# Streaming attention over 8,192 context rows: keys and values kept in DRAM and fetched per unit, 20 block-aligned units in place of 24

## The chip, the cores and the metric

The kernel runs on one core of a Trainium2 chip. The metric is the device time in microseconds. A core has TensorE (PE, with its weight loads PEld), VectorE (DVE), ScalarE (ACT), GpSimd (POOL) and SyncE (SP), which here issues nearly all DMAs; each works through its own queue in order. PE writes its results to PSUM, here in banks of 128 x 512 float32.

## What is computed

The reference is one perceiver layer in float32: a cross attention, a stack of eight linear attention blocks with feed-forward parts, and a sparse feed-forward part. The change touches the cross attention only:

```python
xn = layer_norm(x, gamma_x, beta_x)          # x: 8192 context rows of 512
ln = layer_norm(latents, gamma_l, beta_l)    # 512 latent rows
q = (ln @ Wq).reshape(b, m, h, d)            # 8 heads of 64
k_x, v_x = split(xn @ Wkv);  k_l, v_l = split(ln @ Wkv)
k_x = rope_rotate_k(k_x)
k = concatenate([k_x, k_l]);  v = concatenate([v_x, v_l])
attn = softmax(einsum('bhid,bhjd->bhij', q * scale, k))
out = einsum('bhij,bhjd->bhid', attn, v) @ Wo
```

So 512 queries look at 8,704 keys, in eight heads; the scores don't fit on the chip.

## The kernel before

The heads are taken in four pairs. The 8,704 keys are 17 blocks of 512 (block 0 is that of the latents, 1 to 16 are the context), or 68 chunks of 128. For each pair the softmax is an online one: its 68 chunks are cut into **units**, and behind each unit the running maximum, the weighted sum of values and the sum of exponentials of the pair are brought up to date.

For a block `b`, `fetch_block` loads the rows, `moments_of`, `roots_of` and `centre` normalize them (the root iteration is a chain of small POOL operations), `transpose_rows` turns them on PE, `keys_of(b, j)` projects keys (four pieces j; two pieces make two pairs, multiplied by cosines and sines on DVE, combined on POOL in L254 and L255, and moved by eight small DMAs of SP into the key tiles, L262), and `values_of(b, t)` projects values (four pieces t), which ACT copies out of PSUM in four parts, one for each pair (L270). Keys and values lie in SBUF tiles of 128 x 512 from the pool `x_kv`, which has 27 of them.

For a unit `u` of a pair, in this order:

- `score(u, i)` for its chunks i: two matmuls (pc, one for each head), two copies from PSUM by ACT (L382), and the running maximum over chunks by DVE (mx, L386 and L388). Five PSUM banks (`ps_s`) serve scores, projections and transposes together.
- `maxima(u)`: eight PE transposes (pmx), then reductions by DVE give the new row maxima `mrow`. For a pair that has been met before, POOL takes the difference between old and new maxima (alpha, L406) and ACT its exponential (L407), which is the factor by which the older sums shrink.
- `maxima_rows(u)`: eight PE transposes (mbc) spread the maxima over partitions.
- `exponentials(u, i)`: DVE subtracts (L439), ACT takes the exponential (L440), POOL adds the chunks up (es, L448 and L450).
- `shrink(u)`: eight PE matmuls (pa, L427) spread the factor over partitions, DVE multiplies the older sums `oT` by it (L432).
- `weigh(u, i)`: two PE matmuls (po, L460) weigh the values; behind the last chunk DVE adds to `oT` (L490).
- `sums(u)`: two PE matmuls with ones (pd, L499), then again an addition to `oT`.

The last unit doesn't use es; its sums are formed by PE directly. At a pair's last unit `sums_by_query` and `ones_over` turn the sums into factors (psr, pb), and `project` multiplies by Wo.

The order of all this on PE is written out by hand: the list `steps` holds the chunks, two to a step, 136 steps in all, and the dictionary `todo` holds what else belongs to each step; `rank` sorts the pieces inside a step. `end[u]` is the step of a unit's last scores. Blocks 2 to 16 are spread over eight steps each. The other engines and SP are ordered by the planner of the language, by priority and by the times at which it expects inputs, except where `issue_after` pins an instruction behind another.

Before the change the units grow by 3.25 chunks a time: there are 24 of them, of 4, 6, 9, 12, 12, then mostly 13, and at the end 10, 7 and 4 chunks, and they begin at any chunk of a block.

```python
    STEP = 3.25
    while min(met) < NCHUNK:
        p = k % NPAIR
        upto = min(NCHUNK, int(3 + STEP * k)) if k else 4
```

Of the kernel before, what the change touches and what calls it, by code (L numbers as in the profile page):

```python
# [16 lines left out]
P = 128  # L17
D = 512
# [36 lines left out]
def perceiver_kernel(  # L55
# [85 lines left out]
    kvp = pool("x_kv", 27, stack=xa)  # L141
    sp = pool("x_s", 18, stack=xa)
# [69 lines left out]
    k_sb, v_sb, xT, part, rows_of, trigs = {}, {}, {}, {}, {}, {}  # L212
# [24 lines left out]
    def keys_of(b, j):  # L237
# [18 lines left out]
        for p in (j - 1, j):  # L256
            k_sb[b, p] = kv_tile(f"k{b}_{p}")
            for h in range(2):
                src = slice((p % 2 * 2 + h) * H2, (p % 2 * 2 + h + 1) * H2)
                for i, half_of in enumerate((lo, hi)):  # L260
                    o = h * HD + i * H2
                    nc.sync.dma_start(out=k_sb[b, p][o : o + H2, :], in_=half_of[src, :])  # L262

    def values_of(b, t):
        pv = bank("pv")
        projected(pv, lambda dc: xT[b, dc][:, t * P : (t + 1) * P], lambda dc: wkv[:, 1, dc, :])
        for p in range(NPAIR):
            if t == 0:
                v_sb[b, p] = kv_tile(f"v{b}_{p}")
            nc.scalar.copy(v_sb[b, p][:, t * P : (t + 1) * P], pv[:, p * P : (p + 1) * P])  # L270
# [63 lines left out]
    STEP = 3.25  # L334
    units, met, k = [], [0] * NPAIR, 0
    while min(met) < NCHUNK:
        p = k % NPAIR
        upto = min(NCHUNK, int(3 + STEP * k)) if k else 4
# [16 lines left out]
    for b in range(2, NBLK + 1):  # L355
# [8 lines left out]
        for j, (f, i) in enumerate(pieces, 1):  # L364
            at(begin + j * gap, f, b, i)
        for e, f, *a in normalizing(b + 1) if b < NBLK else ():
            at(begin + e, f, *a)
    at(begin + 8 * gap, values_of, NBLK, TT - 1)
    pieced = set(todo)

    scores, mx, mrow, alpha, mbc, es, po = {}, {}, {}, {}, {}, {}, {}

    def score(u, i):
# [3 lines left out]
        for h in range(2):  # L377
            hs = slice(h * HD, (h + 1) * HD)
            nc.tensor.matmul(pc[h], k_sb[b, p][hs, o : o + P], qT[hs, p, :], start=True, stop=True)  # L379
# [10 lines left out]
    def maxima(u):  # L390
# [13 lines left out]
        if p in mrow:  # L404
            a = alpha[u] = small.tile([P, 2 * TT], F32, tag="alpha", name="alpha", bufs=4)
            nc.gpsimd.tensor_tensor(a, mrow[p], new, ALU.subtract)  # L406
            nc.scalar.activation(a, a, AF.Exp)  # L407
        mrow[p] = new

# [10 lines left out]
    def shrink(u):  # L420

        p = units[u][0]
        pa = bank("pa")
        for qc in range(TT):
            for h in range(2):
                c = h * TT + qc
                nc.tensor.matmul(  # L427
                    pa[h * HD : (h + 1) * HD, qc * P : (qc + 1) * P],
                    alpha[u][:, c : c + 1].to_broadcast([P, HD]), ident,
                    start=True, stop=True,  # L430
                )
        nc.vector.tensor_tensor(  # L432
            oT[p], oT[p], pa.unsqueeze(1).to_broadcast([P, 2, T]), ALU.mult
        )

    def exponentials(u, i, late=False):
# [6 lines left out]
        if i == 1:  # L443
            es[u] = (
                xpool.tile([P, 2, T], F32, tag="es", name="es") if u % 2 or units[u][2] < NCHUNK else
# [6 lines left out]
    def weigh(u, i):  # L452
# [6 lines left out]
        for h in range(2):  # L459
            nc.tensor.matmul(  # L460
                po[u][h * HD : (h + 1) * HD, :],
                v_sb[b, p][:, t * P + h * HD : t * P + (h + 1) * HD],
# [68 lines left out]
    for u, n in enumerate(size):  # L531
        at(end[u], maxima if end[u] in pieced else late_maxima, u)
        at(end[u] + 1, maxima_rows, u)
        if units[u][1]:
            at(end[u] + 2, shrink, u)
        span = size[u + 1] if u + 1 < len(size) else n
        first = last + 1 if u + 2 < len(size) else 0
        for i in range(n):
            d = end[u] + 1 + i * span // n // 2
            at(d, late_exponentials if d in end[-3:] else exponentials, u, i)  # L540
            last = max(d + 1, first)
# [840 lines left out]
```

## Time and profile before

| | us |
|---|---|
| median of three runs (2570.17 to 2570.89) | 2570.39 |
| the profiled execution | 2571.29 |
| its span, first to last instruction | 2569.2 |
| from the first score to the last weighing of the cross attention | 86.32 to about 1211.4 |
| PE, DVE, ACT, POOL busy in 212.15 to 1012.20 | 780, 575, 488, 522 |
| DMA share in that stretch | 0.14 |

In the profile's rows "out<-in" names tiles of the program, "x8" counts instructions merged into one row, and a bracket gives the idle time of the engine before the row and what ended it. A float32 matmul stands in the rows as two instructions, so the two matmuls of a score are "x4"; a transpose is one. A group of 16 "pa" is one shrink.

### The profile page before, as it was taken

The numbers are of one execution on the slowest core, as the hardware profiler recorded it, in microseconds if no ns is written. First come the engines' busy times: TensorE is split into PE (matmuls) and PEld (weight loads), VectorE is DVE, ScalarE is ACT, GpSimd is POOL, SyncE is SP. The second block draws the span as 40 slices with busy tenths as digits, with TensorE's granted clock in tenths as the row PEclk, the third lists the DMA queues.
The fourth block names the chain that finished last, engine by engine and source line by source line (L and its number), as shares of the span: only waits on it lengthen the run. The fifth ranks groups of instructions, "written<-read, shape, count | busy, mean of one in ns | idle before, by whom it ended". The sixth has DMA issues, their size and how long they took to land.

```text
span 2569.2 us, 33740 instructions
## 1 busy us (share of the span) xinstructions
PE 2501.5 (97%) x11560; PEld 1471.0 (57%) x11560; DVE 1746.6 (68%) x3680; ACT 1202.3 (47%) x2285; POOL 1263.4 (49%) x1422
## 2 busy tenths in 40 slices
PE   8999999999999999998999999999999999999998
PEld 4433333334333333333588686886868878687764
DVE  4466767766777776886675767757576575766764
ACT  3465656665566665663433415334153441524303
POOL 0255665666567666775144452544525354263512
PEclk9999999999999999998999999999999999999999
DMA  3111111111111111010522223222222323223235
GB/s 134 42 44 52 29 41 42 42 40 43 34 42 41 42 42 42 9 42 17 193 95 93 72 79 106 95 95 70 95 95 90 95 86 97 92 74 99 66 110 203
DMA packets 98380, 187.49 MB, mean 73 GB/s; under 512 B 10336, under 2 KB 10464, under 8 KB 98208
## 3 DMA queue, kind: packets, MB, share of 16 engines
q1 hardware_dynamic: 88496, 167.29, 20.3%
q10 hardware_dynamic: 8688, 15.94, 2.0%
q0 software_dynamic: 1024, 2.10, 0.3%
q8 instruction: 92, 1.51, 0.2%
q14 instruction: 80, 0.66, 0.1%
HBM read 162.22 MB, written 1.05 MB: 64 GB/s over the span
## 4 chain that ended last, share of the span: by engine, by line
PE 78%; DVE 9%; ACT 5%; issue 4%; POOL 2%; DMA 0%; SPq 0%; DVEq 0%; POOLq 0%; ACTq 0%
PE pb L846 14%; PE ps L635 13%; PE pw L730 9%; PE pv L231 7%; PE pk L231 6%; PE ps L730 6%; PE po L460 6%; PE pc L379 6%; DVE sc L439 4%; PE po L1009 4%; ACT sc L382 2%; ACT sc L440 2%; DVE mx L388 1%; PE pt L218 1%; PE pf L939 1%
## 5 line engine op out<-in xcount | busy, mean ns | idle before, releaser
L450 POOL TENSOR_TENSOR es<-es,sc 128x1024 f32<-128x1024 f32 x222 | 526.1, 2370 | 110.5 <-ACT sc L440 99.9
L388 DVE TENSOR_TENSOR mx<-pc,mx 128x512 f32<-128x512 f32 x448 | 283.3, 684 | 186.5 <-ACT sc L382 186.3
L440 ACT ACTIVATE sc<-sc 128x1024 f32<-128x1024 f32 x272 | 288.4, 1065 | 249.2 <-DVE sc L439 238.1
L382 ACT COPY sc<-pc 128x512 f32<-128x512 f32 x544 | 284.4, 600 | 81.3 <-PE pc L379 67.6
L439 DVE TENSOR_TENSOR sc<-sc,mbc 128x1024 f32<-128x1024 f32 x272 | 319.4, 1209 | 3.7 <-PE mbc L416 2.2
L379 PE MATMUL pc<-qT,k 64*128 64x512 f32 x1088 | 290.9, 621 | 5.8 <-DVE sin L249 2.3
L460 PE MATMUL po<-sc,v 128*64 128x512 f32 x1088 | 263.0, 604 | 0.2 <-DVE mx L388 0.2
L231 PE MATMUL pk<-xn,wkv 128*64 128x512 f32 (+1 forms) x856 | 250.6, 604 | 8.2 <-ACT v L270 3.4
L231 PE MATMUL pv<-wkv,xn 128*64 128x512 f32 (+1 forms) x808 | 248.0, 598 | 7.7 <-DVE sin L249 2.6
L379 PEld LDWEIGHTS pc<-qT,k 64*128 64x128 f32 x1088 | 101.4, 186 | 189.0 <-issue 80.9
L1019 ACT ACTIVATE h<-h,col 128x256 f32<-128x256 f32 x192 | 103.9, 577 | 220.5 <-DVE h L779 151.0
L903 ACT ACTIVATE g<-g 128x512 f32<-128x512 f32 x64 | 39.9, 630 | 344.7 <-DVE g L863 218.7
L730 PE MATMUL pw<-curT,cur 128*128 128x256 f32 (+1 forms) x896 | 177.3, 350 | 0.1
L231 PEld LDWEIGHTS pk<-xn,wkv 128*64 128x64 f32 (+1 forms) x856 | 85.0, 153 | 160.8 <-issue 114.1
L231 PEld LDWEIGHTS pv<-wkv,xn 128*64 128x64 f32 (+1 forms) x808 | 86.6, 155 | 150.8 <-issue 110.8
L812 POOL TENSOR_TENSOR sh<-h 128x128 f32<-128x128 f32 x120 | 83.4, 695 | 176.7 <-PE pb L846 172.1
L986 POOL TENSOR_TENSOR y<-qf,y 128x512 f32<-128x512 f32 x32 | 44.5, 1391 | 243.9 <-DVE y L985 243.9
L730 PEld LDWEIGHTS pw<-curT,cur 128*128 128x128 f32 x896 | 150.2, 190 | 16.9 <-DVE curT L723 0.2
L863 DVE TENSOR_TENSOR g<-g,pb 128x256 f32<-128x256 f32 x135 | 50.0, 417 | 159.7 <-PE pb L846 159.2
L717 POOL TENSOR_TENSOR cur<-w 128x256 f32<-128x256 f32 x128 | 93.5, 741 | 118.5 <-DVE g L904 74.9
L460 PEld LDWEIGHTS po<-sc,v 128*64 128x64 f32 x1088 | 73.6, 138 | 135.2 <-issue 120.0
L846 PE MATMUL pb<-tw,sh 128*128 128x256 f32 x540 | 136.2, 379 | 0.0
(220 smaller groups left out, 4639.7 us busy)
## 6 DMA issues: line engine op xcount, KB each, us to landing
w<-in_wf SPq DMA_DIRECT2D x64, 1024.0 KB, 5.2
k<-cos SPq DMA_DIRECT2D x272, 64.0 KB, 2.0
cb<-in_cx SPq DMA_DIRECT2D x62, 256.0 KB, 3.9
row<-in_rows ACTq DMA_DIRECT2D x48, 256.0 KB, 4.7
f<-in_f SPq DMA_DIRECT2D x10, 1024.0 KB, 5.3
tg<-in_trig SPq DMA_DIRECT2D x16, 512.0 KB, 3.6
wk<-in_wk SPq DMA_DIRECT2D x8, 1024.0 KB, 5.2
wq<-in_wq SPq DMA_DIRECT2D x8, 1024.0 KB, 5.1
```

What stands on the lines that cost most here:

```text
L231: nc.tensor.matmul(ps[o : o + n, :], lhs(dc)[:, o : o + n], rhs(dc), start=(dc == 0), stop=(dc == DC - 1))
L379: nc.tensor.matmul(pc[h], k_sb[b, p][hs, o : o + P], qT[hs, p, :], start=True, stop=True)
L382: copied[0] = nc.scalar.copy(sc[:, h, :], pc[h])
L388: behind[0] = nc.vector.tensor_tensor(mx[u][:, h, :], pc[h], mx[u][:, h, :], ALU.max)
L439: nc.vector.tensor_tensor(sc, sc, mbc[u], ALU.subtract)
L440: nc.scalar.activation(sc, sc, AF.Exp)
L450: nc.gpsimd.tensor_tensor(es[u], es[u], sc, ALU.add)
L460: nc.tensor.matmul(po[u][h * HD : (h + 1) * HD, :], v_sb[b, p][:, t * P + h * HD : t * P + (h + 1) * HD], scores[u, i][:, h, :], start=(i ...
L635: nc.tensor.matmul(ps[:, t0 : t0 + n], w[:, dc, c0 : c0 + P], xT[:, dc, t0 : t0 + n], start=(dc == 0), stop=(dc == DC - 1),)
L730: nc.tensor.matmul(ps, lhs[:, k], rhs[:, k], start=(k == 0), stop=(k == 1))
L846: nc.tensor.matmul(ps[i], lhs, rhs, start=(q == 0 and i in (1, 2, 6, 5, 4)), stop=(q == self.N - 1 and i in (1, 2, 7, 3, 4)),)
L1019: nc.scalar.activation(h, h, AF.Gelu_apprx_tanh, bias=col[:, c : c + 1])
```

## The change

Keys and values are no longer kept in SBUF. Keys go from the rope tiles to DRAM tiles, values are copied by ACT in one instruction into a small tile `vs` and stored to DRAM as well. Each unit loads the key blocks it needs (`load_keys`, three steps before the first score on them) and the value blocks (`load_values`, two steps before the first weighing, in runs of 512 bytes), all by SP. The pool `x_kv` falls from 27 to 9 tiles, and the score tiles rise from 18 to 22.

Units now begin and end at block borders: 20 units of 4, 8 and 12, then fourteen of 16, and at the end 12, 8 and 4 chunks. The number of steps stays 136. With units of 16 the ends and beginnings of units fall on the same two of the eight steps of every block.

The factor: its difference is taken by DVE at the end of `maxima`. The exponential comes a step later, in the new `factor`, which also stores the 128 x 8 factors transposed to DRAM and loads them back twice, each time as one row of 512 broadcast to 64 partitions (`abc`). `shrink` then has no matmuls; DVE multiplies by `abc`. For units of 16 chunks it comes three steps after the unit's end in place of two, for shorter ones two steps after.

The sums and what follows them come a step later (not for the last two units), and the tile es has two buffers. The pieces of the last block come one step earlier, its last values two steps earlier.

```diff
--- before.py
+++ after.py
@@ -138,8 +138,9 @@
     xnp = pool("x_feat", 4, stack=xa)
     cbp = pool("x_rows", 4, stack=xa)
     xpool = pool("xattn", 1, stack=xa)
-    kvp = pool("x_kv", 27, stack=xa)
-    sp = pool("x_s", 18, stack=xa)
+    kvp = pool("x_kv", 9, stack=xa)
+    sp = pool("x_s", 22, stack=xa)
+    dram = pool("x_dram", 1, DRAM, stack=xa)
     ps_s = pool("ps_s", 5, PSUM, stack=xa)
     ps_m = pool("ps_m", 1, PSUM, stack=xa)
     ps_o = pool("ps_o", 1, PSUM, stack=xa)
@@ -209,7 +210,8 @@
     oT = [xpool.tile([P, 2, T], F32, tag=f"oT{p}", name=f"oT{p}") for p in range(2)]
     oT += [x_sb[:, 2 * i : 2 * i + 2, :] for i in range(2)]
     H2 = HD // 2
-    k_sb, v_sb, xT, part, rows_of, trigs = {}, {}, {}, {}, {}, {}
+    k_dr, v_dr, xT, part, rows_of, trigs = {}, {}, {}, {}, {}, {}
+    kt, vt_ = {}, {}
     def transpose_rows(b, dc, gcol, bcol):
         tiles = rows_of[b]
@@ -254,20 +256,33 @@
             nc.gpsimd.tensor_tensor(lo, lo, part["sin1"], ALU.subtract)
             nc.gpsimd.tensor_tensor(hi, hi, part["sin0"], ALU.add)
         for p in (j - 1, j):
-            k_sb[b, p] = kv_tile(f"k{b}_{p}")
+            k_dr[b, p] = dram.tile([P, BLK], F32, name=f"k{b}_{p}")
             for h in range(2):
                 src = slice((p % 2 * 2 + h) * H2, (p % 2 * 2 + h + 1) * H2)
                 for i, half_of in enumerate((lo, hi)):
                     o = h * HD + i * H2
-                    nc.sync.dma_start(out=k_sb[b, p][o : o + H2, :], in_=half_of[src, :])
+                    nc.sync.dma_start(out=k_dr[b, p][o : o + H2, :], in_=half_of[src, :])
     def values_of(b, t):
         pv = bank("pv")
         projected(pv, lambda dc: xT[b, dc][:, t * P : (t + 1) * P], lambda dc: wkv[:, 1, dc, :])
-        for p in range(NPAIR):
-            if t == 0:
-                v_sb[b, p] = kv_tile(f"v{b}_{p}")
-            nc.scalar.copy(v_sb[b, p][:, t * P : (t + 1) * P], pv[:, p * P : (p + 1) * P])
+        vs = tmp.tile([P, D], F32, tag="vs", name="vs", bufs=3)
+        nc.scalar.copy(vs, pv)
+        if t == 0:
+            v_dr[b] = dram.tile([TT, P, D], F32, name=f"v{b}")
+        nc.sync.dma_start(out=v_dr[b][t], in_=vs)
+    def load_keys(u, b):
+        kt[u, b] = kv_tile(f"kt{u}_{b}")
+        nc.sync.dma_start(out=kt[u, b], in_=k_dr[b, units[u][0]])
+    def load_values(u, b):
+        vt_[u, b] = kv_tile(f"vt{u}_{b}")
+        p = units[u][0]
+        nc.sync.dma_start(
+            out=vt_[u, b].rearrange("p (t f) -> p t f", t=TT),
+            in_=v_dr[b][:, :, p * P : (p + 1) * P].rearrange("t p f -> p t f"),
+        )
     wo_last, x_last = [], []
@@ -331,11 +346,10 @@
-    STEP = 3.25
     units, met, k = [], [0] * NPAIR, 0
     while min(met) < NCHUNK:
         p = k % NPAIR
-        upto = min(NCHUNK, int(3 + STEP * k)) if k else 4
+        upto = min(NCHUNK, TT * (k + 1))
         if upto > met[p]:
             units.append((p, met[p], upto))
             met[p] = upto
@@ -362,13 +376,14 @@
         at(begin, *((fetch_block, b + 1) if b < NBLK else (fetch_last,)))
         pieces = *((keys_of, j) for j in range(2)), (values_of, 0), *((keys_of, j) for j in (2, 3)), (values_of, 1), (values_of, 2)
         for j, (f, i) in enumerate(pieces, 1):
-            at(begin + j * gap, f, b, i)
+            at(begin + 1 + (j - 1) * gap, f, b, i)
         for e, f, *a in normalizing(b + 1) if b < NBLK else ():
             at(begin + e, f, *a)
-    at(begin + 8 * gap, values_of, NBLK, TT - 1)
+    made = begin + 7 * gap
+    at(made, values_of, NBLK, TT - 1)
     pieced = set(todo)
-    scores, mx, mrow, alpha, mbc, es, po = {}, {}, {}, {}, {}, {}, {}
+    scores, mx, mrow, alpha, mbc, es, po, abc = {}, {}, {}, {}, {}, {}, {}, {}
     def score(u, i):
         p, c0, c1 = units[u]
@@ -376,7 +391,7 @@
         pc = [ps_s.tile([P, T], F32, tag="s", name="pc") for h in range(2)]
         for h in range(2):
             hs = slice(h * HD, (h + 1) * HD)
-            nc.tensor.matmul(pc[h], k_sb[b, p][hs, o : o + P], qT[hs, p, :], start=True, stop=True)
+            nc.tensor.matmul(pc[h], kt[u, b][hs, o : o + P], qT[hs, p, :], start=True, stop=True)
         sc = scores[u, i] = sp.tile([P, 2, T], F32, tag="s", name="sc")
         for h in range(2):
             copied[0] = nc.scalar.copy(sc[:, h, :], pc[h])
@@ -403,9 +418,21 @@
                 nc.vector.tensor_reduce(new[:, hs], pt, AX.X, ALU.max)
         if p in mrow:
             a = alpha[u] = small.tile([P, 2 * TT], F32, tag="alpha", name="alpha", bufs=4)
-            nc.gpsimd.tensor_tensor(a, mrow[p], new, ALU.subtract)
-            nc.scalar.activation(a, a, AF.Exp)
+            nc.vector.tensor_tensor(a, mrow[p], new, ALU.subtract)
         mrow[p] = new
+    def factor(u):
+        a = alpha[u]
+        nc.scalar.activation(a, a, AF.Exp)
+        line = dram.tile([2 * TT, P], F32, name=f"al{u}")
+        nc.sync.dma_start(out=line.rearrange("c p -> p c"), in_=a)
+        abc[u] = xpool.tile([P, T], F32, tag="abc", name="abc")
+        for h in range(2):
+            nc.sync.dma_start(
+                out=abc[u][h * HD : (h + 1) * HD, :],
+                in_=line[h * TT : (h + 1) * TT, :].rearrange("c p -> (c p)").partition_broadcast(HD),
+            )
     def maxima_rows(u):
@@ -420,17 +447,8 @@
     def shrink(u):
         p = units[u][0]
-        pa = bank("pa")
-        for qc in range(TT):
-            for h in range(2):
-                c = h * TT + qc
-                nc.tensor.matmul(
-                    pa[h * HD : (h + 1) * HD, qc * P : (qc + 1) * P],
-                    alpha[u][:, c : c + 1].to_broadcast([P, HD]), ident,
-                    start=True, stop=True,
-                )
         nc.vector.tensor_tensor(
-            oT[p], oT[p], pa.unsqueeze(1).to_broadcast([P, 2, T]), ALU.mult
+            oT[p], oT[p], abc[u].unsqueeze(1).to_broadcast([P, 2, T]), ALU.mult
         )
     def exponentials(u, i, late=False):
@@ -442,7 +460,7 @@
             return
         if i == 1:
             es[u] = (
-                xpool.tile([P, 2, T], F32, tag="es", name="es") if u % 2 or units[u][2] < NCHUNK else
+                xpool.tile([P, 2, T], F32, tag="es", name="es", bufs=2) if u % 2 or units[u][2] < NCHUNK else
                 xpool.tile([P, 2, BLK], F32, tag="trig", name="es", bufs=1)
             )
             nc.gpsimd.tensor_tensor(es[u], scores[u, 0], sc, ALU.add)
@@ -459,7 +477,7 @@
         for h in range(2):
             nc.tensor.matmul(
                 po[u][h * HD : (h + 1) * HD, :],
-                v_sb[b, p][:, t * P + h * HD : t * P + (h + 1) * HD],
+                vt_[u, b][:, t * P + h * HD : t * P + (h + 1) * HD],
                 scores[u, i][:, h, :], start=(i == 0), stop=(i == c1 - c0 - 1),
             )
         for h in range(2) if u in direct else ():
@@ -532,23 +550,30 @@
         at(end[u], maxima if end[u] in pieced else late_maxima, u)
         at(end[u] + 1, maxima_rows, u)
         if units[u][1]:
-            at(end[u] + 2, shrink, u)
+            at(end[u] + 1, factor, u)
+            at(end[u] + 2 + (n == 2 * TT * 2), shrink, u)
+        begun = end[u] + 1 - n // 2
+        for c in range(0, n, TT):
+            at(max(-1, begun + c // 2 - 3), load_keys, u, (units[u][1] + c) // TT)
         span = size[u + 1] if u + 1 < len(size) else n
         first = last + 1 if u + 2 < len(size) else 0
         for i in range(n):
             d = end[u] + 1 + i * span // n // 2
             at(d, late_exponentials if d in end[-3:] else exponentials, u, i)
             last = max(d + 1, first)
+            if i % TT == 0:
+                b = (units[u][1] + i) // TT
+                at(max(last - 2, made) if b == NBLK else last - 2, load_values, u, b)
             at(last, late_weigh if u == len(size) - 2 and last == end[-1] else weigh, u, i)
-        at(last, sums, u)
+        at(last + (u + 2 < len(size)), sums, u)
         if u == last_of[units[u][0]] and u + 1 < len(size):
-            at(last + 1, sums_by_query, u)
-            at(last + 2, ones_over, u)
-    rank = {maxima_rows: 0, maxima: 2, exponentials: 3, shrink: 4, ones_over: 4, weigh: 5, sums: 6, late_weigh: 6.5, late_maxima: 7, late_exponentials: 8}
-    for d in range(max(todo) + 1):
+            at(last + 2, sums_by_query, u)
+            at(last + 3, ones_over, u)
+    rank = {maxima_rows: 0, maxima: 2, exponentials: 3, factor: 3.5, shrink: 4, ones_over: 4, weigh: 5, sums: 6, late_weigh: 6.5, late_maxima: 7, late_exponentials: 8}
+    for d in range(min(todo), max(todo) + 1):
         behind[1] = behind[0]
-        for s in steps[2 * d : 2 * d + 2]:
+        for s in steps[2 * d : 2 * d + 2] if d >= 0 else ():
             score(*s)
         whole = {maxima, maxima_rows, transpose_rows, sums_by_query}
         halved[0] = not any(f in whole for f, a in todo.get(d, []))
```

## Prediction

> **What bounds the kernel now.** I read the shares of the page first, then the PE timeline of the attention stage step by step, then the waits of the stage, then the DMA issues.
>
> ```profile
> PE 2501.5 (97%) x11560; PEld 1471.0 (57%) x11560; DVE 1746.6 (68%) x3680; ACT 1202.3 (47%) x2285; POOL 1263.4 (49%) x1422
> ...
> PE 78%; DVE 9%; ACT 5%; issue 4%; POOL 2%; DMA 0%; SPq 0%; DVEq 0%; POOLq 0%; ACTq 0%
> ```
>
> TensorE (PE) is nearly always busy, and it holds 78% of the chain of work that ended last. So PE time removed is time removed, as long as nothing else becomes late. The change touches only the attention stage, from the first score at 86.32 us to the last weighing at about 1211.4 us. PE's program order there is written by hand in 136 steps (two chunks of scores each). The PE timeline shows a step without anything extra, from score to score, and the group "pa" of a shrink:
>
> ```profile
> 597.71 1.04 PE L427 MATMUL pa<-ident,alpha 128*64 128x128 f32 x16
> 598.58 1.89 PE L460 MATMUL po<-sc,v 128*64 128x512 f32 x8
> ...
> 664.74 1.99 PE L379 MATMUL pc<-qT,k 64*128 64x512 f32 x8
> 666.65 3.65 PE L231 MATMUL pv<-wkv,xn 128*64 128x512 f32 x16
> 670.14 1.89 PE L460 MATMUL po<-sc,v 128*64 128x512 f32 x8
> 671.95 1.99 PE L379 MATMUL pc<-qT,k 64*128 64x512 f32 x8
> ```
>
> The plain step is 671.95 - 664.74 = 7.21 us, and pa costs 598.58 - 597.71 = 0.87 us. By the same reading (start to next start in this timeline) the eight transposes of the maxima (pmx, 629.84 to 630.80) cost 0.96, those that spread them (mbc, 635.82 to 636.74) 0.92, the two sums matmuls (pd, 652.25 to 653.21) 0.96. A step with the block's transposes is 607.61 to 617.16, 9.55 or 2.34 more than a plain one.
>
> How full is PE? Steps 17 to 111 run from 212.15 to 1012.20:
>
> ```profile
> 212.15:1012.20 800.05, 779.54 (x3435) 297.20 (x3433) 575.39 (x829) 488.15 (x871) 522.05 (x444) 1.00 0.14 40
> ...
> 1121.20:1211.40 90.20, 75.59 (x390) 32.47 (x388) 66.07 (x87) 46.28 (x68) 58.54 (x28) 0.91 0.07 24
> ```
>
> (Columns: stretch, length, then busy time of PE, PEld, DVE, ACT, POOL, the granted clock, DMA share, GB/s.) By the step prices these 95 steps need 95 x 7.21 + 11 x 2.34 + 14 x (0.96 + 0.92 + 0.96 + 0.87) = 763 us. They take 800, so 37 us are lost; about 4 of these are small changeovers (a step with pmx is 8.29, not 8.17), **33 are stalls**. In a list of all steps the loss sits behind the unit ends, up to 5.0 us each. The worst, step 29, in the timeline of all engines:
>
> ```profile
> 303.20 1.99 PE L379 MATMUL pc<-qT,k 64*128 64x512 f32 x8
> ...
> 304.79 2.34 POOL L450 TENSOR_TENSOR es<-es,sc 128x1024 f32<-128x1024 f32 x1
> ...
> 307.24 0.21 POOL L406 TENSOR_TENSOR alpha<-mrow 128x8 f32<-128x8 f32 x1
> ...
> 307.48 0.21 ACT L407 ACTIVATE alpha<-alpha 128x8 f32<-128x8 f32 x1 [6.69 <-POOL alpha L406]
> 307.59 2.03 ACT L382 COPY sc<-pc 128x512 f32<-128x512 f32 x4
> ...
> 309.17 1.29 DVE L386 TENSOR_TENSOR mx<-pc,sc 128x512 f32<-128x512 f32 x2 [6.83 <-ACT sc L382]
> ...
> 317.43 5.34 PE L231 MATMUL pk<-xn,wkv 128*64 128x512 f32 x16 [1.20 <-DVE oT L490]
> ```
>
> The tiny difference alpha (0.2 us) stands on POOL behind an addition and a root iteration. Its exponential stands at the head of ACT's queue and waits 6.69 us; behind it wait the four copies of scores out of PSUM, behind these the maxima on DVE, behind these the banks that PE wants. Then pk takes 5.34 us instead of 3.65: the granted clock was 0.72 in 317 to 323 us. The waits of the stage say how often:
>
> ```profile
> ACT alpha L407 <- POOL alpha L406: 66.6, 16, 8.7
> DVE mx L386 <- ACT sc L382: 61.6, 17, 6.9
> ```
>
> The page "TensorE: Matmul & The Clock Gate" of the Trainium skill (What's actually happening) puts the halved clock behind idle of some 3.4 us; here gaps of about 0.8 and 1.2 us were enough, so the row speaks for more lost by a stall than its idle time. No term below uses the rule.
>
> **Removed PE work.** Units go from 24 to 20, so four times pmx, mbc and pd: 4 x 2.84 = 11.4 us. All 20 pa groups go: 20 x 0.87 = 17.4. Sum 28.8 us. The last stretch (1121 to 1211 us) has PE busy 75.59 of 90.20 and is paced by DVE and ACT chains, so its three pa (2.6) bring nothing: **26 us** on the path.
>
> **Stalls removed.** The difference moves to DVE, right behind the row maxima it needs; its exponential is issued a step later, behind that step's exponentials. So ACT no longer holds the copies. DVE pays 0.2 us 16 times and saves four shrinks (1.21 each) and four pairs of reductions. Sums come a step later with two es buffers: POOL waited 67.9 us for pd in this stretch and no longer must. POOL gets four more additions (249 for 245, 2.37 each, 9.5 us) on 65% of its time. I take two thirds of the 33 us, **22 us**, because the pile-up of subtractions at a unit end remains (a second, mixed cause: bn_stats, rope and gathers ahead in DVE's queue); the ends are 0 and 33.
>
> **Added transfers.** The rows nearest to them:
>
> ```profile
> k<-cos SPq DMA_DIRECT2D x272, 64.0 KB, 2.0
> cb<-in_cx SPq DMA_DIRECT2D x62, 256.0 KB, 3.9
> ...
> cst<-in_consts SPq DMA_DIRECT2D x1, 268.0 KB, 10.6
> ...
> w_c<-in_ctrl SPq DMA_DIRECT2D x1, 128.0 KB, 10.4
> ```
>
> (KB each, median us from issue to landing.) A key load (256 KB, 2 KB rows) is like cb, 3.9 us, and is issued three steps (21.6 us) ahead. A value load has 512 pieces of 512 bytes; between 3.9 and the 10.4 us of w_c (512 pieces of 256 bytes), nearer to cb in bytes, so about 5; it has two steps, 14.4 us. Both hide. The value store (256 KB, as out<-y, 2.3) takes the place of four ACT copies (0.75 us together) by one (0.6). SP pays about 0.5 us an issue: per eight steps 15 more issues, 7.5 us beside some 10.5 now, of 63. DMA share 0.14 leaves room. What can go wrong is order: SP serves its queue in order, and rope stores waited 590.1 us on it for POOL (longest 35.3), but mostly because SP had come early: from rope's last DVE product (662.71) to POOL's last result (668.05) it is 5.3 us. Loads behind these stores still have 8 us or more. I take 3 us in all for late loads, ends 0 and 20 (13 long units, 1.5 us each, like the stalls now).
>
> The factor: exponential 0.2, store of 1024 words of 4 bytes to transposed places, two broadcast loads of 128 KB, then the shrink on DVE, two steps (14.4 us) after. No row shows 4-byte pieces. Below: k<-cos, 2.0 us. Above: w_c by pieces, 1024/512 x 10.4 = 20.8 us. But cst, with larger rows and twice the bytes, landed as late beside it: both sat behind weight loads. So I take 5 us, nearer to k<-cos; loads 2.0 to 4.7 (row<-in_rows, 256 KB); with three issues the chain is 0.2 + 1.5 + 5 + 4 = 11 us: hidden. In the last three units it has one shorter step, but in the old tail alpha was ready at 1189.7 and the shrink ran at 1203.8. Zero, ends 0 and 6.
>
> Against this stands the page "DMA: Bandwidth & Descriptors" (Rules for kernel authors): a strided last dimension becomes one descriptor per element. No run here shows it. By its fixed 2.0 us and 64 packets per engine in 0.67 us my estimate from that page would be 2.7 us, and the sum stays as it is.
>
> Start: the first keys now come by a load. Their stores were issued until 86.06 us, the first score is at 86.32; queued last, the load costs about 5, queued between them nothing: 2 us. Next stage: the pools change size, so the first weights (1 MB, 5.2 us) lie over other tiles; wk was issued at 1126.83 and its first matmul ran at 1231.57, so 0, at worst about 6: 1 us. The last block's pieces one step earlier only reorder PE work: 0, either way 2.
>
> **Sum:** -26 - 22 + 3 + 2 + 1 = -42 us. The profiled execution took 2571.29 us (span 2569.2), 0.9 above the median of 2570.39. So 2571.3 - 42 = 2529.3, by the median 2528.4: I say 2528.5.
>
> **Rivals.**
> (a) Only the work goes; DVE's pile-up at the unit ends keeps PE waiting, and loads cost a little: 2570.4 - 26 + 3 = 2547, from 2540 to 2565. For it: DVE is 72% busy in steps 17 to 111, and waits there name DVE work other than alpha. Against it: unit ends where POOL answered early (step 62, 74) lost only 0.1 us.
> (b) New waits eat all: 2565 to 2575.5, that is, no change (within 0.2%, 5.1 us, about what a measurement can tell).
> (c) **Slower:** the factor's round trip through DRAM ends after the shrink's turn on DVE. DVE then stands, the maxima behind it too, the five banks fill and PE stops. It decides once the chain passes 14.4 us, and the gain of 42 is gone at 3.2 us late in each of 13 long units, that is a store of about 12 us (11 - 5 + 12 = 18). At 20.8 us the chain is 27 us, 12 late, 13 x 12 = 156: 2685. For it: nothing in the trace shows 4-byte pieces. Against: the only small-piece row was as late as its large-piece neighbour.
>
> **How the numbers follow.** Forecast 0.56 (own range 2510 to 2540), (a) 0.24, (b) 0.04, (c) 0.16. Faster by over 0.2% is forecast and (a): 0.80; same 0.04; slower 0.16. The low end is all 33 us of stalls and no new cost (2570.4 - 26 - 33 = 2511, rounded to 2510); the high end reaches through (a) to the edge of no change, 2566, and leaves (c) and most of (b) out.
>
> **What would show it.** Right: no pa group, 20 pmx groups in PE's rows; the wait of ACT for alpha gone; steps 17 to 111 near 760 us; the factor's store landing in 3 to 8 us. Wrong: idle before shrink (line of oT) ended by a DMA; score or po matmuls waiting for a DMA into kt or vt; DVE's idle before mx still ended by ACT's copies as often; first weights late at the stage's end.

## The result and the profile after

The changed kernel takes **2612.6 us** (median of four runs, 2608.55 to 2615.82) against 2570.64 us (median of four runs, 2570.17 to 2571.16). The ratio is **1.0162**, 95% interval 1.0143 to 1.0181: slower. The forecast was 2528.5 us; what happened is what the prediction's rival (c) describes.

The page of the kernel after (busy times; shares of the chain that ended last, by engine and by line):

```profile
PE 2506.9 (96%) x11176; PEld 1451.1 (56%) x11176; DVE 1744.2 (67%) x3676; ACT 1193.1 (46%) x2077; POOL 1269.2 (49%) x1406
...
PE 76%; DVE 8%; DMA 8%; issue 4%; ACT 2%; POOL 1%; SPq 1%; DVEq 0%; POOLq 0%; ACTq 0%
PE pb L871 14%; PE ps L660 13%; PE pw L755 8%; PE pv L233 8%; PE ps L755 6%; PE pc L394 6%; DMA al<-alpha 5%; PE po L478 5%; PE pk L233 4%; PE po L1034 4%; DVE sc L457 3%; DMA abc<-al 2%; PE pt L220 1%; DVE mx L403 1%; PE pf L964 1%
```

A DMA share of 0% has become 8%, and the second row names it: the factor's store (al<-alpha, 5%) and its loads (abc<-al, 2%). A transfer of 4 KB is on the path. PE is even 5.4 us busier than before, with 384 instructions fewer. That is no more work: its records get longer where the granted clock is lower, as shown below.

The same two stretches as before, steps 17 to 111 and the tail, in the kernel after (length, busy PE, PEld, DVE, ACT, POOL, granted clock, DMA share, GB/s):

```profile
207.90:1044.52 836.62, 792.72 (x3170) 284.49 (x3168) 570.53 (x825) 480.85 (x724) 513.95 (x429) 0.96 0.29 86
1158.27:1252.06 93.79, 67.80 (x312) 28.22 (x312) 67.48 (x89) 45.78 (x65) 60.66 (x26) 0.85 0.14 38
```

The 95 steps take 836.6 us, 36.6 longer than before, at a clock of 0.96. The span grew by 44.5 us, and nearly all of it lies in the attention stage: -4.1 in steps 0 to 16, +36.6 in 17 to 111, +4.8 in 112 to 127, +4.4 in the tail; +3.1 lie between the last weighing and the end.

Which wait is it? The waits of the attention stage in the kernel after (sum, times, longest):

```profile
DVE x_sb L450 <- DMA abc<-al: 38.5, 8, 6.4
DVE oT L450 <- DMA abc<-al: 35.0, 7, 7.5
ACT alpha L427 <- DVE alpha L421: 29.6, 13, 4.6
```

`x_sb` and `oT` are the older sums (two pairs each), L450 is the shrink. 15 of the 16 shrinks waited for the factor, 73.5 us together. One of them in the timeline of the kernel after, with its factor's whole way:

```profile
575.73 0.19 DVE L421 TENSOR_TENSOR alpha<-mrow 128x8 f32<-128x8 f32 x1
...
575.96 0.21 ACT L427 ACTIVATE alpha<-alpha 128x8 f32<-128x8 f32 x1 [2.06 <-DVE alpha L421]
...
580.05 0.46 SPq L429 DMA_DIRECT2D al<-alpha  x1
...
591.04 1.09 SPq L432 DMA_DIRECT2D abc<-al  x2
...
591.92 1.03 PE L517 MATMUL pd<-es,ones 128*64 128x512 f32 x4
...
595.06 1.23 DVE L450 TENSOR_TENSOR oT<-oT,abc 128x1024 f32<-128x1024 f32 x1 [7.48 <-DMA abc<-al]
596.20 1.88 DVE L403 TENSOR_TENSOR mx<-pc,mx 128x512 f32<-128x512 f32 x3
...
596.94 3.62 PE L394 MATMUL pc<-qT,kt 64*128 64x512 f32 x6 [4.00 <-DVE mx L403]
```

The difference is there at 575.73, the exponential at 575.96. SP issues a value store, a key load and a value load first, then the factor's store at 580.05. The loads follow 11.0 us later, and the multiplication 4.0 us behind them. DVE had come to it at 587.58 and stood for 7.48 us. The maxima (mx) were queued behind; the scores lacked banks, and PE stood for 4.00 us. The windows view of the 6 us that follow, in the same kernel, shows the granted clock at 0.51:

```profile
597.00:603.00 6.00, 4.88 (x8) 1.90 (x8) 6.00 (x9) 3.56 (x5) 2.56 (x2) 0.51 0.01 1
```

That most of the chain is the store stands in the view of the line that stores the factor, in the kernel after:

```profile
L429 SPq DMA_DIRECT2D al<-alpha x16: 359/406/1583, 295.5 to 1232.8; - x16
...
DMA to landing us min/median/max: 8.8/10.5/11.2
```

1,024 pieces of 4 bytes land in 10.5 us. Little of this is moving them. The windows view of the store shown above, in the kernel after:

```profile
580.00:583.00 3.00, 3.00 (x9) 1.04 (x10) 3.00 (x5) 1.10 (x2) 0.69 (x2) 1.00 0.83 176
583.00:591.00 8.00, 8.00 (x37) 2.60 (x38) 4.58 (x6) 5.07 (x7) 6.75 (x3) 1.00 0.00 0
```

Its packets are over by 583 us; then no DMA engine moves anything (share 0.00) until the store counts as landed, at 591.0. What takes these 8 us no run shows.

The other transfers that the change added or moved are about as cheap as predicted (KB each, median us from issue to landing, kernel after):

```profile
k<-cos SPq DMA_DIRECT2D x272, 64.0 KB, 1.7
v<-vs SPq DMA_DIRECT2D x68, 256.0 KB, 2.1
kt<-k SPq DMA_DIRECT2D x68, 256.0 KB, 4.1
vt<-v SPq DMA_DIRECT2D x68, 256.0 KB, 4.0
```

For the comparisons below I listed all steps of each kernel from PE's rows, from a step's first score to the next one's, and set their sum against the prices of a step's parts (a plain step 7.2 us, and so on). "Extra" is what steps 17 to 111 took above that sum, with pa among the prices in before, e3 and e8, and among the extra in e1 (11 x 0.87 = 9.6 us).

| kernel | time, us | ratio to before (95%) | steps 17-111 | extra | waits for abc |
|---|---|---|---|---|---|
| before | 2570.6 | | 800.1 | 33.5 | |
| after | 2612.6 | 1.0143 to 1.0181 | 836.6 | 90.1 | 73.5 |
| e1_pa | 2521.4 | 0.9789 to 0.9821 | 762.4 | 15.9 | |
| e2_pin | 2527.4 | 0.9814 to 0.9843 | 752.8 | 6.3 | 17.6 |
| e3_dve | 2551.6 | 0.9907 to 0.9937 | 780.6 | 14.0 | |
| e4_row | 2575.8 | 1.0007 to 1.0026 | 803.9 | 57.4 | 0.8 |
| e5_both | **2510.0** | 0.9749 to 0.9776 | 752.8 | 6.3 | 0 |
| e6_place | 2532.0 | 0.9833 to 0.986 | 759.6 | 13.2 | 16.8 |
| e7_flat | 2529.7 | 0.9825 to 0.9852 | 769.1 | 22.6 | 0 |
| e8_units | 2553.2 | 0.9916 to 0.9943 | 782.0 | 15.5 | |
| e9_sums | 2524.2 | 0.9794 to 0.9827 | 763.0 | | |
| e10_act | 2598.1 | 1.0088 to 1.0118 | 826.1 | 79.6 | 58.1 |

(Before stood at 2571.1 us beside e1 to e4 and at 2572.4 to 2572.5 beside the rest.)

In the kernel after, 83.2 of the 90.1 us of extra sit in the second and third step behind a unit's end, in each of the 11 units with a shrink: 5.5 to 10.6 us, on average 7.6. All other steps together have 0.6 us a unit. Of the 84 us by which steps 17 to 111 are longer than in e5, which has one PE instruction more there (its row stands at its experiment below), about half is idle PE (43.9 against 3.5 us) and half is PE busy for longer (792.7 against 749.3 us), at a granted clock of 0.96 in place of 1.00.

### The profile page after: what moved, and what is told of

The parts are those of the page before. It is cut to its first block, busy times and chain, and to the rows that moved or that the text cites. A ratio compares the mean times of both kernels' runs of the same rounds, so it can differ in the third digit from the quotient of the medians.

```text
span 2613.7 us, 33218 instructions
## 1 busy us (share of the span) xinstructions
PE 2506.9 (96%) x11176; PEld 1451.1 (56%) x11176; DVE 1744.2 (67%) x3676; ACT 1193.1 (46%) x2077; POOL 1269.2 (49%) x1406
## 2 busy tenths in 40 slices
DMA packets 173065, 245.19 MB, mean 94 GB/s; under 512 B 30752, under 2 KB 65696, under 8 KB 172896
## 3 DMA queue, kind: packets, MB, share of 16 engines
q0 software_dynamic: 1024, 2.10, 0.3%
## 4 chain that ended last, share of the span: by engine, by line
PE 76%; DVE 8%; DMA 8%; issue 4%; ACT 2%; POOL 1%; SPq 1%; DVEq 0%; POOLq 0%; ACTq 0%
PE pb L871 14%; PE ps L660 13%; PE pw L755 8%; PE pv L233 8%; PE ps L755 6%; PE pc L394 6%; DMA al<-alpha 5%; PE po L478 5%; PE pk L233 4%; PE po L1034 4%; DVE sc L457 3%; DMA abc<-al 2%; PE pt L220 1%; DVE mx L403 1%; PE pf L964 1%
## 5 line engine op out<-in xcount | busy, mean ns | idle before, releaser
L468 POOL TENSOR_TENSOR es<-es,sc 128x1024 f32<-128x1024 f32 x230 | 545.0, 2370 | 298.6 <-ACT sc L458 281.1
L403 DVE TENSOR_TENSOR mx<-pc,mx 128x512 f32<-128x512 f32 x464 | 292.6, 683 | 216.2 <-ACT sc L397 215.9
L394 PE MATMUL pc<-qT,kt 64*128 64x512 f32 x1088 | 299.6, 630 | 43.5 <-DVE sin L251 25.5
L233 PE MATMUL pv<-wkv,xn 128*64 128x512 f32 (+1 forms) x792 | 267.6, 651 | 1.9 <-DVE x_sb L508 1.1
L478 PE MATMUL po<-sc,vt 128*64 128x512 f32 x1088 | 263.7, 605 | 1.1 <-ACT sc L458 1.1
L394 PEld LDWEIGHTS pc<-qT,kt 64*128 64x128 f32 x1088 | 104.1, 188 | 228.7 <-issue 114.8
L755 PEld LDWEIGHTS pw<-curT,cur 128*128 128x128 f32 x896 | 150.2, 190 | 16.8 <-DVE curT L748 0.2
L478 PEld LDWEIGHTS po<-sc,vt 128*64 128x64 f32 x1088 | 73.7, 138 | 147.6 <-issue 134.4
```

The lines of the kernel that those rows point to most:

```text
L233: nc.tensor.matmul(ps[o : o + n, :], lhs(dc)[:, o : o + n], rhs(dc), start=(dc == 0), stop=(dc == DC - 1))
L394: nc.tensor.matmul(pc[h], kt[u, b][hs, o : o + P], qT[hs, p, :], start=True, stop=True)
L403: behind[0] = nc.vector.tensor_tensor(mx[u][:, h, :], pc[h], mx[u][:, h, :], ALU.max)
L468: nc.gpsimd.tensor_tensor(es[u], es[u], sc, ALU.add)
L478: nc.tensor.matmul(po[u][h * HD : (h + 1) * HD, :], vt_[u, b][:, t * P + h * HD : t * P + (h + 1) * HD], scores[u, i][:, h, :], start=(i = ...
L755: nc.tensor.matmul(ps, lhs[:, k], rhs[:, k], start=(k == 0), stop=(k == 1))
```

## The experiments

The theory: the change is good but for the factor's way through DRAM, which ends after DVE has come to the shrink. Its rivals: the DRAM traffic of keys and values costs the time; the new units or the later sums pile up work at the unit ends; or the difference on DVE disturbs DVE.

### e1_pa: the factor by PE again

```diff
-        line = dram.tile([2 * TT, P], F32, name=f"al{u}")
-        nc.sync.dma_start(out=line.rearrange("c p -> p c"), in_=a)
...
+        pa = bank("pa")
...
+                nc.tensor.matmul(
...
-            at(end[u] + 2 + (n == 2 * TT * 2), shrink, u)
+            at(end[u] + 2, shrink, u)
```

> The changed kernel with only the factor's spreading undone: eight PE matmuls (pa) again, two steps after the unit's end, no store and no loads of the factor; difference on DVE, DRAM keys and values, 20 units, late sums as in the change. Theory (the loss is DVE standing in the shrink for the factor's round trip through DRAM, 73.5 us in 15 waits): steps 17 to 111 fall from 836.6 us to about 765 (746.5 of step prices, 12 shrinks of 0.87, 0.6 a unit), the later steps lose some 17 us of waits too, so 2612.6 - 72 - 17 = 2524, from 2518 to 2538. Rival 1 (the added key and value traffic or SP's longer queue is what hurts): the traffic stays, so 2600 or more. Rival 2 (unit ends that always fall on the same steps of a block pile up on DVE): the alignment stays, so 2595 or more, with the loss still five and six steps into each period.

Measured 2521.36 us, 91 less than after. All the rest of the change is still in it: the loads, the units, the later sums, the difference on DVE. Only the factor's way is undone, with the shrink written two steps behind each unit's end, and so the kernel is faster than before. But DVE's turn moved as well: in the long units of steps 17 to 111 the multiplication runs 17.6 us behind the difference, where DVE had come to it after 11.7 us in the kernel after. So e1 alone doesn't tell the way from the turn; e6 changes the turn alone, e7 the way alone. Behind the end of each unit 0.8 us of extra are left in place of 7.6, and that is pa's own time.

### e2_pin: the same round trip, the shrink later

```diff
+        late = units[u][2] - units[u][1] == 4 * TT
+        with tc.issue_after(behind[1].ins) if late else nullcontext():
...
-            at(end[u] + 2 + (n == 2 * TT * 2), shrink, u)
+            at(end[u] + (5 if n == 4 * TT else 2), shrink, u)
```

> The changed kernel with one edit: in the 13 long units the shrink is issued five steps after the unit's end, behind the last maxima of the step before (a fixed place on DVE); store and loads of the factor stay as they are. Theory: the round trip of about 19 us is over by then, DVE doesn't stand, and the 12 long units before step 112 lose 0.6 us in place of about 7.5: steps 17 to 111 near 755, in all 2612.6 - 82 - 7 = 2523, from 2512 to 2532; the tail's three short units keep their waits (4 to 6 us each on DVE). Rival 1 (traffic) and rival 2 (alignment): 2600 or more, since neither is touched. If the store itself slows other transfers, something between.

Measured 2527.36. All transfers are those of the kernel after; only DVE comes later to the long units' shrinks. The timeline of e2_pin, same unit:

```profile
545.91 0.17 DVE L421 TENSOR_TENSOR alpha<-mrow 128x8 f32<-128x8 f32 x1
...
550.41 0.46 SPq L429 DMA_DIRECT2D al<-alpha  x1
...
562.76 1.09 SPq L432 DMA_DIRECT2D abc<-al  x2
...
576.76 1.22 DVE L452 TENSOR_TENSOR oT<-oT,abc 128x1024 f32<-128x1024 f32 x1
```

The store takes no less than in the kernel after (12.4 us from its issue to that of the loads), but the multiplication runs 30.9 us behind the difference, with no bracket: DVE had not waited. So it is not the traffic that costs, but the turn at which DVE needs the factor. 17.6 us of waits remain, all in the three last units, whose shrinks keep their place two steps behind the end.

### e6_place: the turn that the code had meant

The kernel after has its shrink written three steps behind a long unit's end, but the planner put it into the second: DVE reached it 11.7 us behind the difference. Here it is pinned to the written place and nothing else is changed.

```diff
+        late = units[u][2] - units[u][1] == 4 * TT
+        with tc.issue_after(behind[0].ins) if late else nullcontext():
```

> The changed kernel, the shrink in the step in which it is written (three after the end), but in the 13 long units held behind the last maxima of that same step, so that the planner can't put it earlier on DVE. Theory (the change wrote enough distance; the planner moved the shrink up to 12 us behind the difference, against a round trip of 19): DVE gets there 20 to 21 us behind the difference, waits of 0 to 1 us, some 2527, from 2522 to 2540. Rival (three steps are too short wherever it stands): the wait stays 3 us or more a unit, 2560 or more.

Measured 2532.0. In the long units DVE comes 21.1 us behind the difference and waits 0.2 us on average. The factor needs 16.5, so the place that the code had written would have been enough; one step of the planner makes 80.6 of the 91.2 us that lie between the kernel after and e1. The 16.8 us of waits that remain are those of four shrinks, three of them (14.3) at 1107 us and later, where the units are short.

### e7_flat and e4_row: a shorter store

Both store the factors as they lie, 128 runs of 32 bytes, and load the whole 4 KB line into each partition. e4 then multiplies in two halves, reading every eighth word; e7 multiplies once by the first 512 words and leaves out bringing the factors into the order of the queries, so that only its time can be read.

```diff
-        nc.sync.dma_start(out=line.rearrange("c p -> p c"), in_=a)
+        nc.sync.dma_start(out=line.rearrange("(p c) -> p c", c=2 * TT), in_=a)
...
+        for i in range(2):
+            o = oT[p][:, i, :].rearrange("q (c p) -> q c p", c=TT)
+            nc.vector.tensor_tensor(o, o, by_query, ALU.mult)
```

(The last three lines are e4's; e7 has the one multiplication of the kernel after there, reading `flat[:, :T]`.)

> The changed kernel with the fast store (128 runs of 32 bytes) and the loads of the whole line as in the row version, but the shrink is again one multiplication of 128 x 1024 that reads the factor without a stride; it multiplies by factors in the wrong order, so the output isn't the reference's, and only the time is read. Theory (the row version lost its 4.7 us a unit to two strided multiplications of 2.3 us): no wait and no slow multiplication, steps 17 to 111 near 755, in all 2520 to 2535. Rival (the round trip or its larger loads of 256 KB cost by themselves): near the row version, 2560 or more.

> The changed kernel with another layout of the factor in DRAM: the store writes 128 runs of 32 bytes in place of 1,024 pieces of 4 bytes, each load brings the whole line (4 KB) to 64 partitions, and DVE reads it with a stride of 8 in two multiplications. Theory with the number of pieces as the store's price: the store lands in 2 to 4 us in place of 10.5, the chain is some 11 us, DVE gets to the shrink about 11.6 us behind the difference, so it waits 0 to 2 us: 2525, from 2515 to 2545 (the second multiplication and the stride cost at most 2 us a unit on DVE, which has room). Rival (the store's time is the latency of a small write to DRAM or the queue of other transfers, not the pieces): it lands in 8 us or more and the time stays at 2600 or more.

e7 took 2529.7 us. Its store, in the view of the line:

```profile
L429 SPq DMA_DIRECT2D al<-alpha x16: 332/404/1759, 293.9 to 1148.4; - x16
...
DMA to landing us min/median/max: 1.4/2.2/4.1
```

The same 4 KB in 128 pieces land in 2.2 us in place of 10.5. The whole chain takes 6.7 to 11.9 us, and DVE comes to it 10.3 us or more behind the difference, in most long units 11.8, so the factor is there (once 0.1 us late). So the layout of the store alone, too, decides over the time, at the planner's place of the shrink. Steps 17 to 111 took 769.1 us and not the expected 755, though, most likely for the slow multiplication shown below.

**e4 missed**: 2575.8, where 2515 to 2545 was expected. Its waits for abc are 0.8 us in all, so the round trip was hidden, and yet each long unit has 4.7 us of extra. Its two multiplications took 2.3 us each in the median. I had put the cost, if any, on reading every eighth word. But e7 reads without a stride, and its one multiplication is slow as well. The timelines, first e7_flat, then e5_both:

```profile
561.15 5.68 POOL L470 TENSOR_TENSOR es<-es,sc 128x1024 f32<-128x1024 f32 x2
...
562.11 2.50 DVE L452 TENSOR_TENSOR oT<-oT,abc 128x1024 f32<-128x1024 f32 x1
```

```profile
576.33 1.22 DVE L466 TENSOR_TENSOR oT<-oT,abc 128x1024 f32<-128x1024 f32 x1
576.51 5.70 POOL L484 TENSOR_TENSOR es<-es,sc 128x1024 f32<-128x1024 f32 x2 [2.40 <-ACT sc L474]
```

In e7 the multiplication starts inside a POOL addition and takes 2.50 us; in e5 it starts 0.18 us ahead of one and takes 1.22, and POOL's two additions take 5.70 us where two alone take 4.8. In e7 each of the 16 multiplications starts inside such an addition and takes what is left of it plus 1.08 us: 1.42 + 1.08 = 2.50 here, 2.03 + 1.08 = 3.11 at the longest. In the kernel before, DVE read the factor from PSUM and took 1.19 to 1.22 us in all 20 cases, beside POOL or not. The page "SBUF — State Buffer" of the Trainium skill (Who interferes with whom) says that a DVE instruction with two inputs in SBUF contends with a POOL instruction that reads SBUF, and that the shared ports are an exclusive lock, where the order of issue decides who is held up. The rows agree, in both orders. So the greater part of e4's loss is most likely this: a multiplication that meets POOL, twice a unit. One of e4's multiplications without POOL beside it (at 1206.57) took 1.07 us, some 0.4 more than a plain one of its size (0.68); the stride costs that. No kernel was run that takes the stride from e4 and leaves its two multiplications, so how the 4.7 us are divided is argued, not shown.

### e10_act: the store on ACT's queue

In the kernel after SP issues the store 1.4 us behind the exponential on average, in the unit shown because three other issues stand ahead of it. This edit shortens the same chain by a little:

```diff
-        nc.sync.dma_start(out=line.rearrange("c p -> p c"), in_=a)
+        nc.scalar.dma_start(out=line.rearrange("c p -> p c"), in_=a)
```

> The changed kernel with the factor's store issued by ACT's queue, right behind the exponential, in place of SP's. In the changed kernel the store's issue stands 0.2 to 4.1 us (some 2 on average) behind the exponential, since SP first issues a value store and two loads. If DVE's wait is paid one to one, some 2 us in each of 15 waits go: 2612.6 - 30 = 2583, from 2570 to 2600. Rival (the wait is set by the store's pieces and the loads alone, or ACT pays for the issue as much): 2605 or more.

Measured 2598.05. The store leaves 0.1 us behind the exponential and still lands in 10.9 us, so SP's queue was not what made it slow. Waits for abc fall from 73.5 to 58.1 us, by 15.4, and the time by 14.5, half of the 30 expected; 1.4 us an issue were to be had, not 2. The time follows the wait.

### e3_dve: one part of the change alone

The kernel before with the difference on DVE and its exponential a step later; nothing else.

```diff
-            nc.gpsimd.tensor_tensor(a, mrow[p], new, ALU.subtract)
-            nc.scalar.activation(a, a, AF.Exp)
+            nc.vector.tensor_tensor(a, mrow[p], new, ALU.subtract)
...
+            at(end[u] + 1, factor, u)
```

> The kernel before with one edit: the difference of maxima on DVE and its exponential a step later, behind that step's exponentials; 24 units, keys and values in SBUF, pa matmuls as before. The prediction's reading (stalls at unit ends come from ACT waiting for POOL's difference): about 22 of the 33 us of stalls go, 2570.6 - 22 = 2549, from 2538 to 2558, and ACT's wait for alpha is gone. Rival (the pile-up of subtractions at a unit end would keep PE waiting anyway): 2565 or more.

Measured 2551.62: this edit of a few lines brings 19.5 us. The waits from 212 to 1121 us in e3_dve:

```profile
ACT alpha L412 <- DVE alpha L406: 42.7, 16, 5.4
DVE mx L386 <- ACT sc L382: 32.4, 17, 3.5
```

Before, these were 66.6 and 61.6 in the same stretch. ACT's wait for alpha was expected to be gone; it still waits, now for DVE's, but DVE's wait for the copies is halved, and steps 17 to 111 are 19.5 us shorter: the whole gain is there.

### e8_units and e9_sums: units, traffic, later sums

e8 is e1_pa with the 24 old units, so that of the change only the DRAM traffic, the difference on DVE and the later sums remain (and with 16 tiles for keys and values and 18 score tiles); e9 is e1_pa with the sums back in their old step.

```diff
-        upto = min(NCHUNK, TT * (k + 1))
+        upto = min(NCHUNK, int(3 + 3.25 * k)) if k else 4
```

```diff
-        at(last + (u + 2 < len(size)), sums, u)
+        at(last, sums, u)
```

> The pa version of the changed kernel with the 24 units of before (13 chunks, any chunk of a block) in place of the 20; keys and values in DRAM, 16 tiles for them, 18 score tiles, late sums; loads of five blocks a unit where it spans five. It stands against the kernel before with the difference on DVE (2551.6) by the DRAM traffic and the late sums alone, and against the pa version (2521.4) by the units alone. Theory: loads are hidden, so 2551.6 within 5 us, from 2543 to 2557, and the units are worth some 28 (four times pmx, mbc, pd and pa, 3.7 each, is 15, and a part of the stalls in steps that hold two unit or block events). Rival (traffic or SP's order costs): 2560 or more.

> The pa version with one edit undone: the sums (pd) again in the step of the unit's last weighing in place of a step later; es keeps its two buffers. It prices the late sums. Theory (two es buffers already let POOL run on, so PE only now and then waits for the last addition): 2521.4 plus 0 to 8 us. Rival (the late sums carry a good part of the gain over the version with 24 units): 2530 or more.

e8 took 2553.15. Beside e3 (2551.62) it has all the traffic of keys and values more, and the later sums: 1.5 us between them, about what can't be told from nothing. So the rival that blames the traffic falls, to within a few us. Beside e1 (2521.36) it has the old units and the numbers of tiles that go with them: the new ones bring 31.8 us. e9 took 2524.22, so the later sums bring 2.9 us by the medians and 1.5 by the ratios to before; the two intervals overlap, and whether they bring anything stays open.

### e5_both: the fastest

e2's late shrink up to the fifteenth unit, PE's pa matmuls in the last five, where there is no room for a round trip.

```diff
+    PA_FROM = len(size) - 5
...
+        if u >= PA_FROM:
+            pa = bank("pa")
...
+        with tc.issue_after(behind[1].ins) if u < PA_FROM else nullcontext():
...
+            at(end[u] + (5 if u < PA_FROM else 2), shrink, u)
```

> The changed kernel with the shrink of the units up to 14 pinned five steps after the unit's end (factor through DRAM), and pa matmuls two steps after the end in the last five units, where steps are short and the round trip of 19 us showed (DVE waited 17.6 us there in the version that only pins). Theory: steps 17 to 111 as in the pinned version (752.8 us), the rest as in the pa version (108.2 and 80.3): 2521.4 - 762.4 + 752.8 = 2512, from 2508 to 2517, the fastest of all. Rival (the factor's transfers cost PE something even where nothing waits): 2518 or more.

**2510.02 us**, 0.9763 of before. Steps 17 to 111 in e5_both:

```profile
206.30:959.13 752.83, 749.30 (x3171) 274.35 (x3169) 568.63 (x825) 479.96 (x724) 523.75 (x429) 1.00 0.32 95
```

PE is busy 749.3 of 752.8 us at the full clock, with the same DVE, ACT and POOL work as after (836.6 us). There is nothing left in this stretch but PE's own work.

## Why the prediction was wrong

**The step that failed is "the factor", which I took as "hidden" and as "Zero, ends 0 and 6".** Three numbers in it were off, all to the same side:

- The store. "So I take 5 us, nearer to k<-cos": it took 10.5. That lies midway between the two rows taken (2.0 and 20.8), and leaning to k<-cos was the mistake. k<-cos has large pieces; w_c by pieces (20.8 us) was the only row that knew of a price for each piece, and I set it aside since a transfer beside it was as late. The page "DMA: Bandwidth & Descriptors" (Rules for kernel authors), which I had weighed against it, was right that a strided last dimension becomes one descriptor for each element: the kernel after has 30,752 DMA packets under 512 bytes, e7 16,416, and the difference is 16 stores x (1,024 - 128). The same bytes in 128 pieces took 2.2 us. My estimate of 2.7 us from that page's figures fits the moving of the packets (from the issue at 580.05 to 583 us in the unit shown), but not the landing, 8 us later.
- The distance. I counted "two steps (14.4 us)" from the code. The planner had moved the shrink up: DVE came 11.7 us behind the difference in the long units of steps 17 to 111. Chain 16.5, turn 11.7: 4.8 us late. My 11 us chain would have fitted by a hair. At the place that the code had written (21.1 us, e6) even the real chain fits.
- The price of being late. Rival (c), which I gave 0.16, had the mechanism and its place, DVE and the maxima behind it, but not the planner's part: against its turn of 14.4 us the real chain is only 2.1 us late, less than the 3.2 us at which it saw the gain of 42 gone. The real lateness was 4.8 us in a long unit, and the loss was 85 us against e2, 91 against e1 and 103 against e5, which has neither waits nor more than five pa. Each long unit lost 7.6 us for a wait of 4.8. In the 22 such units of the kernel after and e10 the loss exceeds the wait by 0.4 to 5.2 us, on average by 2.9, as much in e10 with its shorter waits: a charge for each stall more than a rate. A part of it is seen: in the unit shown the granted clock fell to 0.51 behind the gap, and the pv that followed at 603.66 took 5.48 us in place of 3.65.

The factor had a fourth cost that I didn't see: the multiplication now reads both inputs from SBUF and meets POOL's additions. In the kernel after the 16 multiplications took 1.22 to 3.09 us, 1.46 in the mean (1.21 before). In e6, in the same unit, it took 2.22 us where e2's took 1.22, and e6 is 4.6 us slower than e2; whether that is the whole reason was not tried.

**The rest of the sum held.** With the factor out of the way, the same parts gave 2521.4 (e1) and 2527.4 (e2) where I had said 2528.5:

- "Removed PE work", 26 us: PE's rows have no pa and 160 pmx, that is 20 groups. e5 and e1 differ in steps 17 to 111 by 9.5 us, 11 times 0.87, just the pa of the 11 shrinks there.
- "Stalls removed", 22 us: e3 shows 19.5 from the difference and its later exponential alone. The copies are freed as predicted, though ACT's wait for alpha is not gone. In e2 and e5 the extra fell from 33.5 to 6.3, so 27 with the units and the later sums.
- "Late loads", 3 us: no PE row of the kernel after waits for kt or vt, and e8 beside e3 gives 1.5 with the later sums. "Start", 2 us: nothing; the first score stands at 86.17 (before 86.32). "Next stage", 1 us: nothing. The weights were issued at 1262.47, behind the last weighing, yet their first matmul runs 20.8 us behind it, before 20.9. The 3.1 us that the rest is longer arise behind the last matmul on wk (211.3 us to the end before, 214.4 in the kernel after, 211.5 in e5), where the code is the same.
- Rival (a), that DVE's pile-up would keep the stalls, falls by e5's full PE.

Of the signs named, the one that decided was right: idle before the shrink's line, ended by a DMA. "The wait of ACT for alpha gone" didn't come: 29.6 us are left in the kernel after, and 29.4 in e5, where PE is full all the same. One sign was badly chosen. "DVE's idle before mx still ended by ACT's copies as often" shows nothing: over the stage L388 and its successor waited 186.3 us before and 186.7 in e5, where PE never stands. DVE waits there because it is early.

## What to carry to other kernels

Here the same 4 KB landed in 10.5 us as 1,024 pieces and in 2.2 us as 128, so a transposing store of single words needs a measured row of its own before it may be called hidden. The distance that hides a round trip is read from the order in which the engine's instructions really ran, not from the step in which the code writes them; where it matters, pin the instruction behind one of the step that is meant. And a wait on an engine in the middle of the pipeline can cost the bound engine more than its length, here 7.6 us for 4.8.

## What the runs showed of the hardware

- 1,024 pieces of 4 bytes from SBUF to DRAM landed in 8.8 to 11.2 us in the kernel after (median 10.5; 10.9 from ACT's queue in e10), 128 pieces of 32 bytes in 1.4 to 4.1 us in e7 (median 2.2). In the store shown, the DMA engines had been idle for the last 8 of the 11 us.
- A DVE multiplication of 128 x 1024 with both inputs in SBUF took 1.22 us alone or when it started first, and when it began inside a POOL addition what was left of that plus 1.08 us, up to 3.11 (e7); with one input in PSUM 1.19 to 1.22 (before).
- The granted clock fell behind short PE gaps: in e4 it was 1.00 from 580 to 586 us and 0.50 from 586.1 to 589.4, behind gaps of 0.4 and 1.6 us; in the kernel after it was 0.50 from 597.2 to 607.3 us, behind gaps of 4.0 and 1.1 us.
